# A computed instruction order whose preferences vary in stretches half as long, twice as many of them

## The chip, the cores and the metric

The kernel runs on one NeuronCore of a Trainium2 chip. The metric is the device time of one execution in microseconds (us), and the number that counts is the median of several executions. In this text PE is the matrix engine (TensorE), PEld its loading of weights, DVE the vector engine, ACT the scalar engine, POOL the GpSimd engine and SP the engine that here only starts transfers. Lines of the kernel are given as L366 for line 366 of the kernel before; in the kernel after, every line below the changed table stands 18 lines lower.

## The reference

The input is x with 8 sequences of 512 tokens and 256 features, all in fp32. The block computes, for every sequence:

```python
x = x + 0.5 * ffn(layernorm(x))     # "half 0"
x = x + ttt(layernorm(x))           # a recurrence over the tokens
x = x + 0.5 * ffn(layernorm(x))     # "half 1"
```

Each `ffn` is a small transformer of two layers (the same weights in both halves). A layer has windowed attention with 8 heads of 64 features (a window of 128 tokens that looks at itself and at the one before, with normalised and rotated queries and keys, and a softmax), an output projection of 512 to 256, and then a gated feed-forward part: a layer norm, a product with `w1` to 2 x 682 features, `a * gelu(g)`, a product with `w2`, and a residual. `ttt` normalises again, makes keys, queries and values, and runs a rank-one update of a 256 x 64 matrix per token, `W = W - 0.01 * (W k - v) k^T`, whose outputs `W q` are added to x.

The 8 sequences do not depend on each other. Within a sequence nearly everything depends on the step before it.

## The kernel before, in words

A sequence is held as 4 windows of 128 tokens, one token to a partition. The recurrence is done in closed form: per sequence, small 64 x 64 products that double an inverse step by step, then a short chain over the 4 windows. All arithmetic is fp32.

No engine's order of work is written out by hand. The functions `sequence`, `attention`, `feed_forward` and `ttt` (L579, L642, L1049, L1245) do not issue instructions; they make nodes. A node is one small group of instructions on one engine (for instance the 4 matmuls of one projection), with a cost in nanoseconds, the nodes it depends on, the buffers that it takes and releases, and a function that issues its instructions. Some nodes may go to either of two engines: the copies out of PSUM to ACT or DVE (L598), the additions of the rotation (L749), the reciprocals (L913) and the shares of the softmax (L923) to DVE or POOL. Up to three sequences are in work at once (the `lane` buffers, L451).

`Scheduler.run` (L361) then plays the program through in planned time and so lists the instructions. It keeps one clock for each engine. In every step it looks at all the nodes whose inputs are planned, works out when each could start, and takes the one with the smallest key, where the key is that start less the node's preference:

```python
stretch = int(self.clock["PE"] // STRETCH)
variation = VARIED[stretch] if stretch < len(VARIED) else 0
...
early = n.early + varied(n.key, variation)
...
key = (t - early + EARLY.get(turn, 0.0) + (cost if len(n.engs) > 1 else 0.0), n.prio)
```

A preference has two parts. The fixed one, `n.early`, comes from the table `EARLY` (L118) by the node's name, stage and sequence. The varied one comes from `varied` (L247). It takes a number `variation` and the node's key (made of its name and its sequence), mixes them, and moves the preference of a quarter of all (name, sequence) pairs by a pseudo-random amount; the others are left alone:

```python
def varied(key, variation):
    x = scramble(key ^ scramble(variation))
    if not variation or x % 4:
        return 0.0
    return ((x >> 8) % 2001 - 1000) * (400, 1000, 2500, 6000)[variation % 4] / 1000.0
```

The remainder of the number by 4 sets how far a preference can move: up to 0.4, 1, 2.5 or 6 us either way. A number of 0 moves nothing. The number in force is read from the table `VARIED`, one number for each stretch of `STRETCH` nanoseconds of PE's planned clock. Beyond the end of the table nothing is varied.

The planner also prices a change of PE's tile shape. Every PE node is of one of three kinds: "full" (128 x 128), "rows" (64 or fewer rows) or "quad" (64 x 64 tiles); a node of another kind than the last is planned later by `PE_DRAIN` of the old kind and `PE_LOAD` of the new one, and its key carries a preference such as `_full_rows` besides. A change of ACT's function table (exp or gelu) is planned at 1313 ns. The transfers are one queue, which SP starts in planned order.

All of this runs while the program is built. On the chip there is only the list of instructions that came out, with a fixed order on each engine and the semaphores between them.

Of the kernel before, what the change touches and what calls it, by code (L numbers as in the profile page):

```python
# [112 lines left out]
def t_pool(n, spread=False):  # L113
# [99 lines left out]

STRETCH = 10000.0
VARIED = [
    11724, 1019, 59022, 40675, 27471, 54517, 926, 43545, 2398, 24437, 2885, 26297, 23063, 34949,
    37569, 50685, 32060, 45684, 31371, 39512, 521, 25144, 9512, 57341, 52812, 27993, 489, 16985,
    33884, 26540, 4908, 18540, 8984, 2421, 40841, 59716, 24566, 55621, 54901, 36686, 11720, 16862,  # L220
    12513, 52674, 46515, 10256, 59276, 45325, 19184, 55405, 46136, 42422, 0, 49317, 40524, 44024,
    17428, 31920, 9589, 43511, 59281, 2218, 23017, 28209, 39306, 27771, 33355, 29993, 985, 13712,
    12640, 23397, 12680, 25585, 54109, 44131, 30596, 53412, 59847, 58748, 23508, 2544, 28302, 26557,
    42944, 35720, 53117, 52196, 48722, 45182, 35154, 35344, 11332, 52827, 37344, 43276, 41480,
    25425, 12724, 27463, 8460, 45364, 1608, 2076, 43844, 20601, 2037, 2469, 59305, 53718, 46665,
    7337, 2226, 52207, 33281, 58457, 21599, 41269, 26533, 7438, 10800, 59668, 36328, 9166, 3745,
    46520, 33573, 21192, 14896, 27355, 52409, 47920, 36060, 3581, 40705, 14777, 12200, 5106, 3270,
    51090, 49236, 40806, 56120, 57783, 44110, 54754, 7737, 4795, 57152, 33780, 10581, 19156, 33936,
    14061, 55609, 27768, 30248, 49510, 51041, 20100, 12337, 22860, 5369, 43128, 56887, 21496, 42396,
    49657, 59934, 54949, 51695, 25315, 48261, 6245, 14319, 39121, 50043, 51556, 33881, 37401, 54689,  # L230
    49233, 9924, 153, 33064, 19456, 55060, 55649, 39006, 35496, 52294, 57662, 8411, 23088, 13299,
    21788, 20784, 0, 45292, 52752, 9077, 52413, 35269, 49088, 4635, 56036, 34956, 34764, 55744,
    11631, 10468, 37148, 21711, 44697, 28554, 26398, 22219, 1471, 23536, 6706, 44201, 48828, 45578,
    39704, 45276, 44363, 20013, 25017, 14320, 36906, 53273, 39761, 9386, 19064, 51436, 46401, 15636,
    47446, 53601, 57004, 17096, 7331, 58485, 46128, 47692, 33874, 15433, 23706, 38397, 0, 31180,
    20101, 11661, 56899, 1609, 28145, 25749, 31949, 39204, 1318, 18757, 46711, 24881, 52292, 1629,
    38037,
]


# [72 lines left out]
class Scheduler:  # L313
# [47 lines left out]
    def run(self):  # L361
        ready = [n for n in self.nodes if n.left == 0]
        left = len(self.nodes)
        while left:
            best = None
            stretch = int(self.clock["PE"] // STRETCH)  # L366
            variation = VARIED[stretch] if stretch < len(VARIED) else 0
# [1389 lines left out]
```

## Time and profile before

| | |
|---|---|
| median of 3 executions | 2679.28 us (2678.38 to 2680.19) |
| profiled execution | 2681.69 us, of which the span from the first to the last instruction is 2679.9 us |
| PE busy | 2635.3 us, 98% of the span, 30128 matmul records |
| PEld / DVE / ACT / POOL busy | 1995.6 / 1846.5 / 1650.8 / 1543.8 us |
| granted PE clock | 0.999 |
| transfers | 44.61 MB in all, 4.8% of the 16 engines' span on the main queue |

PE is busy nearly all the time. PE's busy time is a modelled one, since the end of a matmul is worked out and not observed, so a busy PE can still lose time between two matmuls. A matmul in fp32 leaves two records.

### The profile page before, as it was taken

Reading aid. Unit: us, or ns where it says so; the run is one execution under the profiler, and the core shown is the slowest. Engines: PE = TensorE matmul, PEld = TensorE weight load, DVE = VectorE, ACT = ScalarE, POOL = GpSimd, SP = SyncE. Lnnn points to the kernel's source line nnn. Section 1 sums busy time; section 2 is a strip of 40 time slices with the busy share of each in tenths; the row PEclk is TensorE's granted clock in tenths of the full one; section 3 lists DMA queues with packets and bytes.
Section 4 is the critical chain, followed back from the end, with each engine's and each line's share of the span. In section 5 each row is a group of like instructions: output and inputs, shape, how many; then the busy total and the mean of one; then the engine's idle time right before and its main releaser. Section 6 shows DMA issues by size and latency. Waiting matters only on the chain.

```text
span 2679.9 us, 75965 instructions
## 1 busy us (share of the span) xinstructions
PE 2635.3 (98%) x30128; PEld 1995.6 (74%) x30128; DVE 1846.5 (69%) x5571; ACT 1650.8 (62%) x4342; POOL 1543.8 (58%) x2153
## 2 busy tenths in 40 slices
PE   8999999999999999999999999999999999999998
PEld 4777777777767777777777777777777777777776
DVE  6767757765777667766776777776777756776755
ACT  5666665755666666666565666657656656556554
POOL 7655655654576466656565656457556645456633
PEclk9999999999999999999999999999999999999999
DMA  5000000000100000000000000000010000000000
GB/s 184 9 9 16 7 6 17 11 6 6 32 6 10 8 24 17 8 8 9 8 29 8 10 9 24 18 8 8 9 30 8 10 7 8 9 24 8 8 13 17
DMA packets 58554, 44.61 MB, mean 17 GB/s; under 512 B 7468, under 2 KB 55768, under 8 KB 58200
## 3 DMA queue, kind: packets, MB, share of 16 engines
q1 hardware_dynamic: 58200, 39.77, 4.8%
q8 instruction: 237, 3.88, 0.6%
q14 instruction: 117, 0.96, 0.1%
HBM read 18.79 MB, written 4.19 MB: 9 GB/s over the span
## 4 chain that ended last, share of the span: by engine, by line
PE 92%; DVE 2%; DMA 2%; POOL 2%; ACT 1%; issue 1%; SPq 0%; DVEq 0%; POOLq 0%; ACTq 0%
PE ps L1124 22%; PE ps L690 17%; PE ps L1215 9%; PE ps L1031 8%; PE ps L777 8%; PE ps L841 6%; PE ps L980 6%; PE ps L943 4%; PE ps L801 3%; PE ps L638 3%; PE ps L1424 2%; PE ps L1226 1%; PE ps L1336 1%; DMA hs<-x 1%; PE ps L1568 1%
## 5 line engine op out<-in xcount | busy, mean ns | idle before, releaser
L1124 PE MATMUL ps<-h2T,w 128*128 128x256 f32 (+1 forms) x2816 | 646.1, 381 | 2.6 <-DVE gT L1165 1.3
L1124 PEld LDWEIGHTS ps<-h2T,w 128*128 128x128 f32 (+1 forms) x2816 | 521.3, 188 | 122.5 <-issue 30.6
L690 PE MATMUL ps<-wqkv,hT 128*128 128x512 f32 x1024 | 490.2, 603 | 1.4 <-DVE x L1349 1.1
L896 ACT ACTIVATE pr<-pr,s 128x192 f32<-128x192 f32 (+1 forms) x1024 | 440.4, 433 | 49.9 <-DVE s L884 45.8
L917 POOL TENSOR_TENSOR pr<-pr,s 128x384 f32<-128x384 f32 (+1 forms) x375 | 293.5, 790 | 283.9 <-DVE s L909 260.8
L726 POOL TENSOR_TENSOR st<-st,powc 128x8 f32<-128x8 f32 x256 | 438.2, 1712 | 21.3
L884 DVE CUSTOM_DVE_ANT_0 pr<-ps,amask,st 128x192 f32<-128x192 f32 (+1 forms) x1024 | 360.8, 394 | 44.4 <-PE ps L841 36.0
L911 POOL TENSOR_TENSOR s<-s,powc 128x2 f32<-128x2 f32 x189 | 133.7, 708 | 342.5 <-ACT pr L896 341.2
L1165 DVE SCALAR_TENSOR_TENSOR gT<-ps,b,gl 128x256 f32<-128x256 f32 x320 | 151.0, 482 | 219.6 <-PE ps L1124 189.1
L690 PEld LDWEIGHTS ps<-wqkv,hT 128*128 128x128 f32 x1024 | 185.4, 191 | 154.5 <-issue 137.0
L1215 PE MATMUL ps<-w,gT 128*128 128x256 f32 x1280 | 291.4, 379 | 0.3 <-DVE s L884 0.3
L1215 PEld LDWEIGHTS ps<-w,gT 128*128 128x128 f32 x1280 | 241.6, 190 | 50.8 <-issue 15.3
L709 ACT ACTIVATE tmp<-ps 128x512 f32<-128x512 f32 x256 | 152.4, 597 | 174.0 <-DVE rot L734 127.0
L734 DVE TENSOR_TENSOR rot<-ps,rt 128x512 f32<-128x512 f32 x256 | 175.7, 688 | 117.4 <-PE ps L690 103.8
L1031 PE MATMUL ps<-wo,oT 128*128 128x256 f32 x1024 | 244.0, 381 | 0.5 <-DVE oT L1024 0.5
L777 PE MATMUL ps<-wqkv,hT 128*128 128x512 f32 x512 | 240.5, 594 | 0.0
L1031 PEld LDWEIGHTS ps<-wo,oT 128*128 128x128 f32 x1024 | 190.7, 190 | 51.2 <-issue 19.2
L602 ACT COPY prT<-ps 128x512 f32<-128x512 f32 (+1 forms) x364 | 176.9, 548 | 58.6 <-PE ps L943 56.5
L1146 ACT ACTIVATE gl<-ps,b 128x256 f32<-128x256 f32 x320 | 140.8, 473 | 105.9 <-PE ps L1124 101.1
L841 PE MATMUL ps<-kT,qT 64*64 64x128 f32 (+1 forms) x7168 | 194.2, 251 | 9.7 <-ACT qT L602 8.3
L980 PE MATMUL ps<-prT,v 64*64 64x128 f32 (+1 forms) x7168 | 197.1, 247 | 6.1 <-DVE prT L602 2.9
L746 POOL TENSOR_TENSOR rot<-rot,tmp 128x512 f32<-128x512 f32 x146 | 185.4, 1273 | 19.6 <-DVE tmp L740 14.8
(123 smaller groups left out, 4372.5 us busy)
## 6 DMA issues: line engine op xcount, KB each, us to landing
hs<-x SPq DMA_DIRECT2D x128, 64.0 KB
hs<-x SPq DMA_DIRECT2D x128, 63.5 KB
base<-in_x_dram SPq DMA_DIRECT2D x8, 512.0 KB
out_dram<-base SPq DMA_DIRECT2D x8, 512.0 KB
w<-in_w_dram SPq DMA_DIRECT2D x6, 640.0 KB
x<-in_x_dram SPq DMA_DIRECT2D x7, 512.0 KB
wqkv<-in_wqkv_dram SPq DMA_DIRECT2D x2, 1024.0 KB
hs<-x SPq DMA_DIRECT2D x96, 0.5 KB
```

What stands on the lines that cost most here:

```text
L690: nc.tensor.matmul(pp.ap, hT[w].ap[:, c * P : (c + 1) * P], wqkv[:, c, i * INNER : (i + 1) * INNER], start=(c == 0), stop=(c == 1),)
L726: nc.gpsimd.tensor_tensor(ss, ss, powc[:, 0:HEADS], ALU.pow)
L746: (nc.vector if e == "DVE" else nc.gpsimd).tensor_tensor(rot.ap, rot.ap, tmp.ap, ALU.add)
L777: nc.tensor.matmul(pv.ap, hT[w].ap[:, c * P : (c + 1) * P], wqkv[:, c, 2 * INNER : 3 * INNER], start=(c == 0), stop=(c == 1),)
L841: nc.tensor.matmul(sc[par].ap[half(c), k * 4 * DH + at : k * 4 * DH + at + keys.stop - keys.start], qT.ap[half(par), 2 * g + k, half(c)], ...
L884: nc.vector.tensor_tensor_reduce(out=pr(k, nj), in0=sc.ap[:, k * 4 * DH : k * 4 * DH + nj], in1=amask[:, 0:nj] if w else amask[:, 3 * DH : ...
L896: nc.scalar.activation(pr(k, nj), pr(k, nj), AF.Exp, bias=st.ap[:, k : k + 1], scale=-1.0, accum_out=st.ap[:, 2 + k : 3 + k],)
L917: (nc.vector if e == "DVE" else nc.gpsimd).tensor_tensor(both, both, st.ap[:, 4:6].unsqueeze(2).to_broadcast([P, 2, nj]), ALU.mult)
L980: nc.tensor.matmul(po[r].ap[half(par), k * P + first : k * P + first + cols * DH], v[j].ap[half(r), hd * DH : (hd + 1) * DH], prT.ap[half( ...
L1031: nc.tensor.matmul(py.ap[:, 0:D], oT.ap[:, c, :], wo[:, c, :], start=(c == 0), stop=(c == INNER // P - 1))
L1124: nc.tensor.matmul(dst.ap[0:rows, 0 : 2 * P], w1[:, kc, col : col + rows], h2T.ap[:, kc, :], start=(kc == 0), stop=(kc == 1),)
L1215: nc.tensor.matmul(py.ap[:, 0:D], gT.ap[:, at : at + P], w2[:, c, :], start=(c == 0), stop=False)
```

## The change

The length of a stretch goes from 10000 to 5000 ns of PE's planned clock, and the table gets new numbers: 530 instead of 266. Nothing else is edited: the nodes, their instructions, their costs, the fixed preferences, the buffers, and `varied` itself are the same.

```diff
-STRETCH = 10000.0
+STRETCH = 5000.0
 VARIED = [
-    11724, 1019, 59022, 40675, 27471, 54517, 926, 43545, 2398, 24437, 2885, 26297, 23063, 34949,
...
-    20101, 11661, 56899, 1609, 28145, 25749, 31949, 39204, 1318, 18757, 46711, 24881, 52292, 1629,
-    38037,
+    54413, 41150, 14171, 39649, 52402, 36490, 5549, 10839, 48709, 17782, 21656, 10404, 9224, 35468,
...
+    6330, 24948, 14409, 34389, 22667, 43373, 33894, 54086, 37257, 28926, 6550, 31300, 31124,
 ]
```

The numbers after are not the numbers before, each written twice: three values occur in both tables. By their remainders 0, 1, 2 and 3 (moves of up to 0.4, 1, 2.5 and 6 us) the table before has 102, 91, 39 and 34 numbers, the table after 144, 126, 145 and 115. The table before has three zeros, the table after none.

## The prediction

> **What bounds the kernel now.** I read the page first, for the engines and the slices:
>
> ```profile
> span 2679.9 us, 75965 instructions
> PE 2635.3 (98%) x30128; PEld 1995.6 (74%) x30128; DVE 1846.5 (69%) x5571; ACT 1650.8 (62%) x4342; POOL 1543.8 (58%) x2153
> PE   8999999999999999999999999999999999999998
> PE 92%; DVE 2%; DMA 2%; POOL 2%; ACT 1%; issue 1%; SPq 0%; DVEq 0%; POOLq 0%; ACTq 0%
> ```
>
> PE is the bound throughout: 98% busy, no slice between the first and the last below nine tenths, and 92% of the chain that ended last. No other engine is over 69%. So the change matters only as far as it moves one of three things on PE: the time before its first and after its last matmul, idle time between matmuls, and time lost inside "busy" when the tile shape changes.
>
> Next the busy time by stretches, to place the idle time (after the stretch's bounds come its length and PE's busy time):
>
> ```profile
> 20.00:335.00 315.00, 310.02 (x3515) 228.62 (x3517) 226.15 (x689) 198.38 (x540) 206.35 (x274) 0.99 0.09 28
> 335.00:670.00 335.00, 328.67 (x3835) 251.47 (x3826) 216.31 (x656) 203.56 (x528) 183.76 (x259) 1.00 0.03 9
> ...
> 1340.00:1675.00 335.00, 334.74 (x3820) 255.88 (x3822) 238.89 (x720) 212.03 (x556) 200.04 (x282) 1.00 0.05 16
> 1675.00:2010.00 335.00, 334.44 (x3906) 254.78 (x3899) 238.03 (x718) 212.07 (x555) 187.26 (x261) 1.00 0.05 14
> ```
>
> PE's idle time is length less busy. Over the eight stretches from 20 to 2670 us it is 4.98, 6.33, 3.68, 4.90, 0.26, 0.56, 2.94 and 7.76, together 31.4 us. The first 20 us add 7.9 and the last 10 us 5.3: the loads ahead of the first matmul (7.39 us) and the last addition and store. The reader should see that 670 us in the middle hold 0.8 us of idle time, while the same work elsewhere idles up to 6.3 us per 335.
>
> The waits of PE show that no single cause stands behind the 31 us:
>
> ```profile
> PE ps L841 <- ACT qT L602: 8.3, 14, 1.5
> PE ps L638 <- DVE x L629: 7.9, 3, 7.4
> PE ps L801 <- POOL rot L746: 3.4, 3, 2.7
> PE ps L980 <- DVE prT L602: 2.9, 6, 0.7
> PE ps L980 <- ACT prT L602: 2.7, 5, 1.2
> ```
>
> The 7.9 is the start. The rest is short waits at the scores (L841), the turns (L801) and the weighted sums (L980) of attention: the chain from one small group to the next came back too late, with nothing else put between.
>
> The timeline of PE shows the third thing, an excursion to small tiles and back:
>
> ```profile
> 303.89 4.48 PE L1124 MATMUL ps<-h2T,w 128*128 128x256 f32 x20
> 308.30 1.21 PE L943 MATMUL ps<-sq,pr 64*128 64x64 f32 x32
> 309.34 0.66 PE L801 MATMUL ps<-sq,rot 64*128 64x64 f32 x16
> 310.16 1.68 PE L980 MATMUL ps<-prT,v 64*64 64x128 f32 x64 [0.16 <-ACT prT L602]
> 311.66 1.05 PE L841 MATMUL ps<-kT,qT 64*64 64x128 f32 x32
> 312.65 0.70 PE L690 MATMUL ps<-wqkv,hT 128*128 128x512 f32 x1
> ```
>
> Here the order has put two turns and two quad groups of different work side by side, so that four groups pay for one excursion (three changes: full to rows, rows to quad, quad to full). I counted the changes over PE's whole timeline: 571 (154 full to rows, 73 back, 69 full to quad, 149 back, 103 rows to quad, 23 back). From the last start before a change to the first start after it, less the usual distance of the group that was left (216 ns for the 256-column matmuls, whose change to rows takes 310 ns in the median), they cost 87.2 us together, 0.153 us each. A few of them contain an idle wait, so this and the idle time overlap a little.
>
> From the first to the last matmul there are 2667.2 us (7.4 to 2674.6); less 31.9 idle and 87.2 for changes, 2548 us are plain streaming. That part is the same in any order. Some 118 us depend on the order.
>
> **What the Trainium skill says.** The page "TensorEngine Tiling (Array Packing)", section "Key Properties", says that changing the tiling mode, and not just the tile, drains TensorE. The trace agrees: a change costs 0.09 us (310 less 216) to 0.15 us more than a step within the shape. The page "Perfetto Trace Analysis", section on the tensor engine's instruction, says that the end of a matmul is computed; the trace agrees, since records at a distance of 216 ns have a mean length of 381 ns (L1124). So I count changes by starts and not by gaps. The page "ScalarE: Activation LUTs", section "What ACT_TABLE_LOAD costs", gives 1283 ns for a load and 2.66 us for a whole switch; the trace has 182 loads of 1283 ns each, 233.5 us on ACT, and nothing here shows the larger figure.
>
> **The change part by part.**
> 1. Instructions: none is added or taken away on PE, whose nodes are the same; 30128 records stay. The varied preference is worked out while the program is built: 0 us on the chip. Transfers are the same in number and size; only their place in the queue can move.
> 2. Assignment: copies may move between ACT (548 ns mean, L602) and DVE, the rotation's addition and the shares between DVE and POOL (790 ns, L917). With ACT at 62%, DVE at 69% and POOL at 58% busy these are covered by PE; uncovered, one such copy late is at most a wait like those above (1.5 us at the longest after the start, but for L801's 2.7).
> 3. ACT's table loads: the count may move. Ten more or fewer are 12.8 us on an engine that is idle for about 1000 us. Hidden, unless a load falls before a copy of qT that PE awaits; those waits are 8.3 us in all now.
> 4. Changes of shape: 0.153 us for each one more or fewer. This is fully on the path, since PE has no cover.
> 5. PE's idle time: bounded below by what the best stretch shows. At 0.26 us per 335 all 2650 us would idle 2.1, a gain of 29.3. Bounded above by the rate of the stretch from 335 to 670: 6.33 x 2650/335 = 50.1, a loss of 18.7.
> 6. Start and end: the first draws act on loads that all come before PE starts; 7.4 us stay. The end could move by about 1 us of its 5.3.
>
> The trace of before cannot tell where between these ends the new order lies. So I take a value from the code. The planner reads one number per stretch of PE's planned clock, so the two tables reach to 266 x 10 = 2660 and 530 x 5 = 2650 us. If each table is as long as the plan that it steers, which the code does not force, PE's planned end before lies between 2650 and 2660, and after between 2645 and 2650. Against 2674.6 in the trace, a plan of that size is believable: the chip would be 15 to 25 us longer. The difference of the plans is then between 0 and -15 us, with its middle at -7.5. I take that, and carry it over one to one, since what a plan can save (changes and idle time) is time on the chain, of which PE has 92%. It needs little of the 118 us: 6%, for example 25 fewer changes of 571 (3.8 us) and 3.7 us less idle.
>
> Sum: span 2679.9 - 7.5 = 2672.4; with the 1.8 us around it (2681.69 - 2679.9) 2674.2 for a profiled execution. The median of the runs is 2.4 below that execution (2679.28 against 2681.69), so the forecast is 2671.8 us, 0.28% less.
>
> **The rivals.** 0.2% is 5.4 us, about what a measurement of this kernel can tell from no change.
>
> A, the forecast: the plan is shorter and the chip follows, by 5.4 to 16 us, so 2663 to 2674. For it: the lengths of the tables, and that a preference which holds for 5 us can be right for one excursion (8.8 us from 303.9 to 312.7, with its full part) without being wrong for the next.
>
> B, no change: the plan is shorter by a few us only, or the chip fills the places which the plan emptied, because its waits come from delays that the plan prices alike for all nodes. 2674 to 2684, middle 2678. For it: the chip spends 15 to 25 us that the plan would not know, and an unknown of that size need not be equal in two orders; a quarter of it is 5 us.
>
> C, slower, by one mechanism: larger moves. The limits of the moves, weighted by the remainders, are on average (102 x 400 + 91 x 1000 + 39 x 2500 + 34 x 6000)/266 = 1629 ns before and (144 x 400 + 126 x 1000 + 145 x 2500 + 115 x 6000)/530 = 2332 ns after. A quarter of the pairs is pulled 43% further from its fixed preference, so a group of turns comes earlier or later than its copies; on the chip, where a copy is not exactly on its planned time, PE then stands at L841 or L980. It decides from 5.4 us on: 17% more idle time than 31.4, or 36 more changes. With idle time half way to the bound of step 5 (+9) and 20 more changes (+3) it is +12, so 2691; 2685 to 2699. Against it: the planner sees the same larger moves, and would have shown most of their harm in its own clock.
>
> D, the numbers do not do what the change's shape suggests: they are not fitted to this plan. For it: their remainders are nearly even (144, 126, 145, 115), as draws fitted to nothing would be, where before small moves are three times as frequent as large ones. Then PE would lose order everywhere: changes up by a quarter (+22) and idle time at the rate of the worst stretch (+19) is +41, so 2720; 2700 to 2760. Against it: 530 numbers, not 532, and a plan worse by 41 us would have wanted some 540 for its length.
>
> **How the numbers follow.** A 0.50, B 0.27, C 0.13, D 0.10. Faster by over 0.2%: A, 0.50. Within: B, 0.27. Slower: C and D, 0.23. A's own range is 2663 to 2674. The range for 8 in 10 is 2661 to 2694: it leaves out a little of A's lower end (0.04), the upper part of C (0.05) and D (0.10).
>
> **What would show it.** Right: 30128 PE records again, the streaming part near 2548 us, fewer than 571 changes of shape and less than 31.4 us of idle time from 20 us to ten us before the end, with DVE, ACT and POOL within some 10 us of their busy times. Table loads may differ from 182 without an effect. B: changes and idle time move in opposite ways. C: the changes about equal, but the waits at L859 and L998 (now L841, L980) longer. D: changes above 650 and idle time spread over all stretches, the 670 good us in the middle gone. The forecast is wrong if the tables are not as long as their plans, or if the plan's error on the chip differs between the two orders by more than the 7.5 us.

## The result

The kernel after takes 2692.68 us (median of 6 executions, 2691.8 to 2696.38), the kernel before 2679.45 us beside it. The ratio is 1.0051 with a 95% interval of 1.0038 to 1.0064: 13.2 us slower, where 7.5 us faster had been forecast. The time lies inside the stated range, near its upper end, and on the other side of no change.

The page of the kernel after, with the same lines as before the change (share of busy time by engine, PE by slices, the chain that ended last):

```profile
span 2692.7 us, 75931 instructions
PE 2639.6 (98%) x30128; PEld 1997.6 (74%) x30128; DVE 1861.7 (69%) x5591; ACT 1656.7 (62%) x4316; POOL 1563.9 (58%) x2179
PE   8999999999999999999999999999999999999998
PE 89%; DVE 3%; POOL 2%; ACT 2%; DMA 2%; issue 1%; SPq 0%; DVEq 0%; POOLq 0%; ACTq 0%
```

PE is the bound as before and has the same 30128 records. Its share of the chain fell from 92% to 89%. Three points are some 80 us, far more than PE's idle time grew by (8.8 us, below): the share says where the chain runs, and not how long PE stood.

The stretches (bounds, length, PE's busy time, then the other engines):

```profile
20.00:335.00 315.00, 305.03 (x3684) 220.66 (x3683) 221.68 (x682) 202.91 (x550) 203.64 (x264) 1.00 0.09 28
335.00:670.00 335.00, 331.39 (x3682) 255.28 (x3681) 224.07 (x665) 200.26 (x513) 183.76 (x272) 1.00 0.03 9
...
1340.00:1675.00 335.00, 330.65 (x3893) 250.26 (x3892) 239.25 (x726) 212.85 (x551) 204.73 (x284) 0.99 0.06 18
1675.00:2010.00 335.00, 332.77 (x3796) 255.26 (x3795) 234.10 (x708) 211.57 (x544) 200.04 (x276) 1.00 0.05 13
```

The first stretch idles 10.0 us (4.98 before), the good 670 us in the middle 6.6 (0.8 before). From PE's first to its last matmul the records give 2680.2 us, 13.0 more than before. Of these, 40.7 are idle (31.9 before) and 85.6 are lost at 564 changes of shape (87.2 at 571). The remaining 2554 us of streaming are 6 more than before. Taken from start to start within one shape, with the idle time in it, the whole loss lies among the 64 x 64 tiles: their steps took 408.8 us against 390.7, those of the row shape 234.3 against 237.0, those of the full shape 1885.3 against 1886.0.

So the changes of shape fell a little, as forecast, and the idle time rose. The waits of PE say on whom (line that waited, tile and line waited for, us in total, times, longest):

```profile
PE ps L859 <- ACT qT L620: 14.3, 23, 2.0
PE ps L656 <- DVE x L647: 7.4, 3, 6.8
PE ps L998 <- DVE prT L620: 5.7, 6, 1.4
PE ps L1142 <- ACT gl L1164: 2.1, 2, 1.0
```

The scores (L859) wait 14.3 us for copies of qT, against 8.3 before, and the weighted sums (L998) 5.7 us for copies of prT, against 2.9.

**Where the chip leaves the plan.** `Scheduler.run` keeps a planned start for every node, and its last clock can be read when the program is built. This is the planner's own arithmetic and no measurement of the chip. It ends at 2659.6 us before and at 2649.7 after, 9.9 us less. It lists 571 and 564 changes of shape and 182 and 202 table loads, as many as the traces hold. So the inference from the lengths of the tables was right: the new order is shorter in the plan. The chip ended 19.8 us above the plan before, and 43.0 after.

I set each PE node's planned start against the start of its first record and looked where the distance grows. The 192 weighted sums of windows with a neighbour stand out. From their start to the next node's start the chip took 0.4 us more than the plan before, summed over all of them, and 19.6 us more after. The cases lie together, a little after certain turns of queries and keys (a turn is their transpose on PE, L819; kT, qT and prT are the turned keys, queries and softmax shares, copied out of PSUM). This is one, in the kernel after: the timeline of PE, then of ACT, then of DVE. In brackets is the idle time before, and what ended it.

```profile
793.95 0.66 PE L819 MATMUL ps<-sq,rot 64*128 64x64 f32 x16
...
795.05 0.84 PE L998 MATMUL ps<-prT,v 64*64 64x128 f32 x30
797.33 0.90 PE L998 MATMUL ps<-prT,v 64*64 64x128 f32 x32 [1.44 <-DVE prT L620]
798.94 0.59 PE L859 MATMUL ps<-kT,qT 64*64 64x128 f32 x8 [0.71 <-ACT qT L620]
```

```profile
793.70 1.07 ACT L620 COPY prT<-ps 128x512 f32<-128x512 f32 x2 [1.06 <-PE ps L961]
795.97 0.59 ACT L620 COPY kT<-ps 128x512 f32<-128x512 f32 x1 [1.19 <-PE ps L998]
798.30 0.59 ACT L620 COPY qT<-ps 128x512 f32<-128x512 f32 x1 [1.74 <-PE ps L998]
```

```profile
794.20 0.69 DVE L620 COPY prT<-ps 128x512 f32<-128x512 f32 x1
796.59 0.69 DVE L620 COPY prT<-ps 128x512 f32<-128x512 f32 x1 [1.69 <-ACT kT L620]
```

The turn (L819) is done before 794.7, yet the copy that takes kT out of PSUM waits for a weighted sum (L998) with which it has no data in common. The second copy of prT on DVE then waits for that copy of kT, again without common data. PE, which needs that prT, stands for 1.44 us; then the copy of qT waits for the next weighted sum, and PE stands for 0.71 us more.

The code shows what they share. A turn writes two PSUM banks, and each of its two copies reads both with one instruction. `slots` prefers two banks side by side and takes any two if there are none. `both_of` then addresses them as `banks[:, low : high + 1 : high - low, :]`. Here the two were banks 0 and 7, and the groups in between lay in banks 1 to 6. In the plan a copy is bound to its two banks alone. The built program binds it to work in the banks that it strides over: this copy of kT carries semaphore waits for the weighted sum in banks 3 and 6 and for DVE's copy of prT out of bank 2, and DVE's copy of prT out of bank 1 waits for the copy of kT. In the whole kernel after, 24 of the 32 copies of turns with banks apart wait for work that was listed after their turn (13 of 20 before), and of the copies of turns with neighbouring banks none does (0 of 224, and 0 of 236 before). The waits are thus written into the program; that the chip itself would need them is not shown. The Trainium skill, page "PSUM — Partial Sum Buffer", section "PSUM bank collisions raise a hardware error", says that accesses of two engines to one bank have to be ordered, reads too. The wait of DVE's copy for ACT's (1.69 us above) keeps two reads apart in this way, but in a bank that ACT's copy steps over and does not read, for which the page asks no order. Of the 128 turns, 10 have their banks apart before and 16 after. In the 6 us after these turns the chip falls behind the plan by 12.3 us before and by 23.4 us after.

### The profile page after: what moved, and what is told of

It is laid out like the page before. It is cut to its first block, busy times and chain, and to the rows that moved or that the text cites. A ratio compares the mean times of both kernels' runs of the same rounds, so it can differ in the third digit from the quotient of the medians.

```text
span 2692.7 us, 75931 instructions
## 1 busy us (share of the span) xinstructions
PE 2639.6 (98%) x30128; PEld 1997.6 (74%) x30128; DVE 1861.7 (69%) x5591; ACT 1656.7 (62%) x4316; POOL 1563.9 (58%) x2179
## 4 chain that ended last, share of the span: by engine, by line
PE 89%; DVE 3%; POOL 2%; ACT 2%; DMA 2%; issue 1%; SPq 0%; DVEq 0%; POOLq 0%; ACTq 0%
PE ps L1142 22%; PE ps L708 15%; PE ps L1233 9%; PE ps L1049 8%; PE ps L795 7%; PE ps L998 6%; PE ps L859 6%; PE ps L961 4%; PE ps L819 3%; PE ps L656 2%; PE ps L1442 2%; PE ps L1244 1%; PE ps L1354 1%; DMA x<-in_x_dram 1%; POOL st L744 1%
## 5 line engine op out<-in xcount | busy, mean ns | idle before, releaser
L935 POOL TENSOR_TENSOR pr<-pr,s 128x384 f32<-128x384 f32 (+1 forms) x397 | 308.5, 784 | 256.0 <-DVE s L927 241.7
L620 ACT COPY prT<-ps 128x512 f32<-128x512 f32 (+1 forms) x346 | 167.6, 542 | 89.7 <-PE ps L961 80.0
L764 POOL TENSOR_TENSOR rot<-rot,tmp 128x512 f32<-128x512 f32 x155 | 197.2, 1276 | 31.9 <-DVE tmp L758 28.0
L859 PE MATMUL ps<-kT,qT 64*64 64x128 f32 (+1 forms) x7168 | 195.6, 252 | 14.5 <-ACT qT L620 14.3
L998 PE MATMUL ps<-prT,v 64*64 64x128 f32 (+1 forms) x7168 | 197.6, 248 | 8.6 <-DVE prT L620 5.7
```

Of the source, the lines that this page charges most:

```text
L764: (nc.vector if e == "DVE" else nc.gpsimd).tensor_tensor(rot.ap, rot.ap, tmp.ap, ALU.add)
L859: nc.tensor.matmul(sc[par].ap[half(c), k * 4 * DH + at : k * 4 * DH + at + keys.stop - keys.start], qT.ap[half(par), 2 * g + k, half(c)], ...
L935: (nc.vector if e == "DVE" else nc.gpsimd).tensor_tensor(both, both, st.ap[:, 4:6].unsqueeze(2).to_broadcast([P, 2, nj]), ALU.mult)
L998: nc.tensor.matmul(po[r].ap[half(par), k * P + first : k * P + first + cols * DH], v[j].ap[half(r), hd * DH : (hd + 1) * DH], prT.ap[half( ...
```

## Experiments

The theory (F) is thus: copies that stride over foreign banks are ordered against those banks' work, which the plan doesn't know. The rivals are C and D of the prediction (larger moves; numbers that are not fitted), and a second cause (T), table loads of ACT that the plan puts into idle time and the program behind a wait.

**One instruction per bank, in the kernel after.** The order stays the planned one.

```diff
+def apart(e, i, dst, pts, whole):
+    at = sorted(v.slot[3] for v in pts)
+    if at[1] - at[0] == 1:
+        return whole(e)
+    for r in range(2):
+        (nc.scalar.copy if e == "ACT" else nc.vector.tensor_copy)(
+            dst.ap.rearrange("p g (r t) -> p r g t", r=2)[:, r],
+            banks[:, at[r], i * 4 * DH : (i + 1) * 4 * DH].rearrange("p (g t) -> p g t", g=4),
+        )
```

> The kernel after, with the same planned order, but where the two PSUM banks of a turn of queries and keys do not lie side by side (16 of the 128 turns) the two copies that read them are written as two instructions each, one per bank, instead of one instruction that strides over the banks between. Theory F (a copy that strides over foreign banks is ordered after the matmuls and before the copies of those banks, and PE then waits for it; the planner doesn't know): the 23 us by which the chip falls behind the plan in the 6 us after these 16 turns mostly go; 2672 us (2668 to 2680), and PE's waits for qT fall from 14 us to about 4. Rival C (larger moves make every copy a little late, far banks are chance): 32 more instructions and nothing gained, 2690 to 2696. Rival D (numbers not fitted): as C.

Measured: 2664.92 us (2663.97 to 2666.34), a ratio to the kernel before of 0.9943 (0.9926 to 0.9959). That is 27.8 us less than the kernel after, and below the band that was expected (2668 to 2680). The same place in its timeline (L852 is the split copy, L1011 the weighted sum, L872 the scores):

```profile
785.12 0.66 PE L819 MATMUL ps<-sq,rot 64*128 64x64 f32 x16
785.37 1.29 DVE L620 COPY prT<-ps 128x512 f32<-128x512 f32 x2
...
785.83 0.67 ACT L852 COPY kT<-ps 128x256 f32<-128x256 f32 x2
...
786.23 1.45 PE L1011 MATMUL ps<-prT,v 64*64 64x128 f32 x60
786.36 0.69 ACT L852 COPY qT<-ps 128x256 f32<-128x256 f32 x2
...
787.57 1.51 PE L872 MATMUL ps<-kT,qT 64*64 64x128 f32 x62
```

The copies of kT and qT now follow each other at once and beside the weighted sums, the copies of prT run together, and PE goes through. The waits of PE in this kernel:

```profile
PE ps L656 <- DVE x L647: 7.5, 3, 7.0
PE ps L872 <- ACT qT L620: 2.1, 10, 0.5
PE ps L1155 <- ACT gl L1177: 2.1, 2, 1.0
```

The wait for qT went from 14.3 to 2.1 us, and PE's idle time between its first and last matmul from 40.7 to 20.0 us. That is 20.7 of the 28.5 us by which the time between these two matmuls fell (2680.2 to 2651.8 us); the rest came out of time that the modelled records count as busy. The steps among the 64 x 64 tiles went from 408.8 to 384.0 us. None of the copies at the 16 turns now waits for work listed after its turn, and in the 6 us after these turns the chip falls behind the plan by 0.3 us in all. F holds. C falls as the cause of the loss: the moved preferences and their order are the same, and the loss is gone.

**The same edit in the kernel before.**

> The same edit in the kernel before, where 10 of 128 turns have banks apart and the chip falls 12 us behind the plan after them. Theory F: 2669 us (2666 to 2673), about 10 us faster than before. Rivals C and D: no change, 2678 to 2682. If F is the whole cause of the loss, this kernel is slower than the kernel after with the same edit by the plan's 9.9 us; if F is half of it, the two are within 5 us of each other.

Measured: 2670.43 us (2667.76 to 2671.27), ratio 0.9963 (0.9948 to 0.9978): 9.0 us less, and idle time from 31.9 to 21.8 us. The same mechanism costs the kernel before a third as much, at 10 turns instead of 16. With the edit on both sides the new numbers win by 5.5 us, between the two cases that the expectation named.

**Half a dose.** The edit at the first 8 of the 16 turns alone.

```diff
-    if at[1] - at[0] == 1:
+    if at[1] - at[0] > 1 and pts not in far:
+        far.append(pts)
+    if at[1] - at[0] == 1 or far.index(pts) >= 8:
         return whole(e)
```

> The kernel after with split copies at the first 8 of the 16 turns with banks apart alone (those up to 1103 us). In the trace of after, the chip fell behind the plan by 11.0 us after these 8 and by 12.4 after the other 8; splitting all 16 gave 27.8 us. Theory F: each turn costs by itself, so 11.0/23.4 of 27.8, 13 us less than after: 2680 us (2676 to 2684). A rival in which a few turns carry all, or in which an early gain is lost again later: under 2672 or over 2688 us.

Measured: 2679.26 us (2678.5 to 2680.71), 13.4 less than the kernel after, where 13 had been expected. Half of the turns carry about half of the cost, so no single place makes it.

**The edit at all 128 turns.** The test `if at[1] - at[0] == 1` with its return is taken out.

> The kernel after with the copies of all 128 turns written as two instructions, not of the 16 with banks apart alone. If splitting itself gave the 28 us (shorter reads, an earlier release), this gives more: under 2660 us. Theory F: nothing to gain at the other 112, and 224 more instructions on ACT and DVE, 2663 to 2670 us.

Measured: 2665.65 us (2665.01 to 2666.25), as with the 16 alone. Shorter reads are not what gives the time.

**An activation ahead of each table load, in the kernel after.** The table is loaded for this small activation, which waits for nothing.

```diff
+            if turn == "_table":
+                self.warm(n.kind)
             n.emit(eng)
...
+    spare = const.tile([P, 2], F32, name="spare")
+    sch.warm = lambda kind: nc.scalar.activation(
+        spare[:, 1:2], spare[:, 0:1], AF.Exp if kind == "exp" else AF.Gelu
+    )
```

> The kernel after, with the same planned order, and a 1-column activation of the wanted function on a private tile ahead of each of the 202 activations that change ACT's function table, so that the table load no longer stands behind the wait of the activation that needs it. Theory T (part of the loss is table loads that the plan puts into ACT's idle time and the chip behind a wait; ACT is idle 23.4 us before loads after, 14.1 before): PE's waits for gl fall, 2688 us (2684 to 2691). If loads are no part of it: 2692 to 2697, since 202 more activations of about 0.2 us cost ACT 40 us of idle time.

Measured: 2689.74 us (2686.16 to 2690.58), 2.9 less than the kernel after. The groups of table loads, first of the kernel after and then of this one (count, busy us, mean ns, idle time of ACT before them):

```profile
L914 ACT ACT_TABLE_LOAD x100 | 128.3, 1283 | 8.2 <-DVE s L902 6.6
L1164 ACT ACT_TABLE_LOAD x82 | 105.2, 1283 | 10.3 <-PE ps L1142 5.8 <-DVE x L647 1.6 <-issue 1.5
L1203 ACT ACT_TABLE_LOAD x19 | 24.4, 1283 | 4.9 <-PE ps L1142 2.4 <-issue 1.7 <-DVE oT L1042 0.5
```

```profile
L496 ACT ACT_TABLE_LOAD x201 | 257.9, 1283 | 3.5
```

The idle time before loads fell from 23.4 to 3.5 us. So some loads had stood behind the wait of the activation that needs them, although the plan lets them begin as soon as ACT is free. The built program shows where: in the kernel after, 58 of the 202 loads follow a separate wait instruction of the activation that needs them; in this one none does. PE's 2.1 us of waits for gl are gone from the list.

**Both edits, after and before.**

> Both edits in the kernel after. If both theories hold and add up: 2668 us (2663 to 2674). F alone: as the kernel after with split copies, within 2 us, or up to 3 us more for the added activations.

> Both edits, the split copies of turns with banks apart and the activation ahead of each table load, in the kernel before. The plan's own clocks end 9.9 us apart. If the two causes found are nearly all of what kept the chip from following the plan, this kernel takes 2669 us (2666 to 2672), 7 to 10 us more than the kernel after with both edits (2660.9). If something else in the order after costs the chip time too, the two are within 4 us.

Measured: 2660.94 us (2659.9 to 2662.54; ratio 0.993, 0.9915 to 0.9944) for the kernel after, 2668.92 us (2667.59 to 2671.05; ratio 0.9955, 0.9938 to 0.9972) for the kernel before. The first is below the band that was expected (2663 to 2674), as its first edit alone had been. The second edit gives 4.0 us more after and 1.5 before. The 4.0 is clear of the spread; the 1.5 is not, since the two runs it is taken from overlap and were made on different chips. In the kernel before, ACT had been idle for only 14.1 us before loads:

```profile
L896 ACT ACT_TABLE_LOAD x90 | 115.5, 1283 | 4.0 <-DVE s L884 2.5
L1146 ACT ACT_TABLE_LOAD x79 | 101.4, 1283 | 3.3 <-DVE x L629 1.3 <-PE ps L1124 0.4 <-issue 0.3
L1185 ACT ACT_TABLE_LOAD x12 | 15.4, 1283 | 6.8 <-PE ps L1124 3.9 <-DVE gT L1165 1.2 <-issue 0.8
```

With both edits on one chip, side by side:

> The kernel after with both edits once more, on the same chip as the kernel before with both edits, to compare the two directly: the plans' clocks end 9.9 us apart. 2661 us; 8 us (5 to 10) under the kernel before with both edits.

> The kernel before with both edits, beside the kernel after with both: 2669 us. If the two edits have removed what kept the chip from following, 5 to 10 us over the other; if the two are within 3 us, the first comparison was chance.

Measured: 2661.05 us (2660.25 to 2662.34; ratio 0.9927, 0.9915 to 0.994) and 2669.88 us (2666.91 to 2670.98; ratio 0.9957, 0.9944 to 0.9969). With both causes out of the way, the new numbers are worth 8.8 us, of the 9.9 that the plans' clocks differ by. The kernel after with both edits is the fastest here, 18.7 us under the kernel before.

**The same numbers shuffled, and none.** The table of the kernel after in a random order, and an empty one.

> The kernel after with the same 530 numbers in a shuffled order. Rival D (the numbers are not fitted to this plan): the time of the kernel after, within some 30 us. If they are fitted: the planner's own clock ends at 3057 us, 407 us later, with 1070 changes of shape instead of 564, and the chip follows to about 3075 us (3060 to 3100).

> The kernel after with an empty table, so that only the fixed preferences act. The planner's own clock ends at 2752.7 us, with 667 changes of shape, and 1 of the 128 turns has its banks apart instead of 16. Theory F (the chip falls behind the plan mostly after such turns): the chip ends 10 to 16 us above the plan, like the two kernels with split copies (10.8 and 15.2), so 2763 to 2769 us. Rival (an order off the plan's model costs the chip more at any rate, 20 us before and 43 after): 2773 to 2796 us.

Measured: 3055.5 us and 2746.05 us, one execution each. Their pages begin:

```profile
span 3053.7 us, 75855 instructions
PE 2826.2 (93%) x30128; PEld 2054.0 (67%) x30128; DVE 1892.2 (62%) x5611; ACT 1676.8 (55%) x4371; POOL 1489.9 (49%) x2094
```

```profile
span 2744.2 us, 76045 instructions
PE 2671.9 (97%) x30128; PEld 2005.6 (73%) x30128; DVE 1860.9 (68%) x5571; ACT 1621.5 (59%) x4315; POOL 1557.0 (57%) x2160
```

The shuffled numbers cost 362.8 us against the kernel after, with 1070 changes of shape and 212.8 us of idle time on PE. Rival D falls: the numbers are fitted to their places. Both runs missed the band stated for them, on the low side: the chip ends 1.6 us below the plan with shuffled numbers and 6.7 us below it with none. The four kernels with a fitted order (two orders, each without and with both edits) all end above their plans:

| kernel | plan's last clock | chip | chip less plan |
|---|---|---|---|
| no numbers | 2752.7 | 2746.05 | -6.7 |
| after, shuffled | 3057.1 | 3055.5 | -1.6 |
| before | 2659.6 | 2679.45 | +19.8 |
| after | 2649.7 | 2692.7 | +43.0 |
| before, both edits | 2659.6 | 2669.9 | +10.3 |
| after, both edits | 2649.7 | 2661.1 | +11.3 |

Banks apart are no mark of the fit itself. With no numbers there is 1 such turn of 128, with shuffled ones there are 12, in fitted tables 10 and 16. With 213 us of idle time in PE's order, 12 such turns may hide, where a fitted order leaves little to hide them; no run splits the copies in the shuffled order, so this is a guess. It also stays open why both fitted orders, with both causes out, still end 10 to 11 us above their plans, and the unfitted ones below.

## Why the prediction was wrong

The loss adds up from the runs. The shorter plan gives -9.9 us, by the planner's arithmetic (the chip shows -8.8 once both edits are in). Banks apart cost 27.8 us after and 9.0 before, +18.8. Table loads behind waits cost 4.0 and 1.5, taken with the first edit in place, +2.5, of which the 1.5 is within the spread. That is +11.4 of the measured 13.2; the other 1.8 us are not explained, and are about as large as the spread of the executions.

**What held.** PE as the bound; the counts of records; the streaming part, but only to 6 us, though it had been called "the same in any order"; the 118 us that hang on the order, within which all of this took place; the reading of the tables' lengths as the lengths of the plans (9.9 us shorter, 7.5 assumed); changes of shape fewer (564), worth 1.6 us in the trace. The gain itself was real: 8.8 us, once the two causes are out. That the time lies inside the range is luck: the upper part of the range was there for rival C, whose reason did not hold.

**The step that failed** is the last of the part-by-part sum: "I take that, and carry it over one to one, since what a plan can save (changes and idle time) is time on the chain." The saving was read as time on PE, which it is in the plan; but an order is good in the plan for its exact times, and the chip adds waits that the plan has no term for. The chip's excess over the plan was 19.8 us before and 43.0 after, and copies bound to banks that they step over make 9.0 and 27.8 of it. The text had an excess of 15 to 25 us before its eyes for the kernel before, called it believable, and took it as the same for both; its last sentence names this as a way to be wrong, and the difference is 23.2 us where 7.5 were enough.

**Steps 2 and 3** were too confident. A late copy was bounded by "at most a wait like those above" (1.5 us, or 2.7 once). The longest wait for a copy in the new trace is 2.0 us, which lies between the two, but one late copy made the next one late, and there were 16 such places instead of 10. Table loads were called hidden "unless a load falls before a copy of qT"; the waits for qT stayed at 14.3 us with the loads moved forward, and what went were PE's 2.1 us of waits for the gelu of the feed-forward (gl). Loads were worth some 3 to 4 us in the kernel after.

**The rivals.** C named nearly the right time (2691) and the right waits (scores and weighted sums, with the changes of shape about equal), but for a wrong reason. With the copies split on both sides, the order with the larger moves is 5.5 us faster. Whether larger moves make banks fall apart more often is not shown; the same moves in a shuffled order gave 12 such turns, against 16. B had the right kind of reason, "delays that the plan prices alike for all nodes", and its sign came true (fewer changes, more idle time), but it allowed the reason a size of 5 us; it was over 20. D had the even remainders for it, which proved to be no evidence: with the same remainders shuffled, the kernel takes 362.8 us more.

**The evidence that was there.** The trace before already held the wait that matters, in the view of all engines' waits: copies of kT that wait for something other than their turn.

```profile
ACT kT L602 <- PE ps L801: 174.8, 79, 6.5
ACT kT L602 <- PE ps L980: 6.4, 3, 2.8
ACT kT L602 <- PE ps L943: 6.1, 3, 2.6
ACT kT L602 <- PE ps L1424: 3.1, 1, 3.1
```

Only the first of these is a dependence of the data: a copy of kT needs its turn (L801), and none of the products of the other three lines. In the kernel after the wait for the weighted sums is 11.7 us in 8 cases.

## What to carry to other kernels

A searched order is only as good as the planner's list of what must wait for what: before trusting a planned gain of 0.4%, look in the trace for waits between instructions that share no data, and mend those first. Here the mend was to read two PSUM banks with two instructions when they are not neighbours, and in the kernel after it was worth more than the new numbers (27.8 us against 8.8). And the distance of chip and plan in one fitted order is no constant that can be carried to the next.

## What was not expected of the hardware

A copy of 512 columns that strides from one bank to another far one takes no longer than others: on ACT, the 28 copies of kT and qT at the turns with banks apart took 587 ns in the mean in the kernel after, and the 216 at neighbouring banks 591 ns. All its cost is in the waits around it, and these are the program's. And a table load of 1283 ns can stand behind the wait of the activation that needs it: ACT was idle for 23.4 us before such loads, and for 3.5 us when a one-column activation with nothing to wait for came ahead of each. That activation took 203 ns in the mean, 41.0 us for all 202, and the kernel was still faster.
